# Last convolution of a four-layer network: one image loaded by nine transfers from two queues instead of three from one

## The chip, the cores and the metric

The kernel runs on one core of a Trainium2 chip. The metric is device time in microseconds (us) of one execution, as the median of several; lower is better.

## What is computed

Four layers in a row on a tensor of 8 images x 16 channels x 256 x 256 in float32; each layer adds its output to its input after a group normalisation:

```python
x = x + _L0_conv_ref(_gn(x), ...)   # 3x3 convolution, then three routing rounds
x = x + _L1_conv_ref(_gn(x), ...)   # 3x3 spline convolution
x = x + _L2_conv_ref(_gn(x), ...)   # attention over 16x16 patches
x = x + _L3_conv_ref(_gn(x), L3_conv_weight)
```

Only the last layer is touched. Its reference is written with Fourier transforms and amounts to a 3x3 convolution with circular borders, 16 channels in and 16 out, on each of the 8 images:

```python
Lw = jnp.fft.fft2(w_pad * dL)
Kx = jnp.fft.ifft2(x, norm='ortho')
z = jnp.einsum('oihw,bihw->bohw', Lw, Kx)
y = jnp.fft.fft2(z, norm='ortho')
```

## The kernel before

The layers run one after another. Layer 2 leaves each image in a DRAM scratch tensor, x3[b], with its rows padded to 258 elements (WP). Layer 3 (layer3, from L1474) loads an image into an SBUF tile of 128 partitions x 33 row groups x 258 floats, 34,056 bytes per partition, convolves it there and stores the result to the output.

Layer 3 runs over the 8 images in order, and each image in two halves, s = 0 and s = 2. A half is 384 matmuls of 32x32 weights on 512 columns (products, L1512 to L1526), each with its own weight load, all unrolled: 768 pairs of weight load and matmul per image, 6144 in the layer. The normalisation is folded into the weights ws, which weights (L1500) makes for the next image. At the end of a half ScalarE and VectorE move the sums from PSUM to a tile y (evict, L1528); y has four buffers. Then store (L1539) issues 12 or 13 transfers of a half's 2 MB, those of row blocks 0 and 1 on SyncE's queue and those of 2 and 3 on GpSimd's (L1545).

An image is loaded by fetch3 (L1466): two transfers of 16 row groups each over all 128 partitions (16,512 contiguous bytes per partition, L1471), and one small one (L1472). The first image goes into a buffer x30 during layer 2, issued by SyncE (first3, L1396, called at L1391). The other seven are issued by ScalarE (fetch, L1496). Images 1 and 2 are issued one after the other at the start of the layer (L1570, L1571). Image n + 2 takes the buffer of image n - 1, and is issued in image n between its two halves, for n = 1 to 5 (L1575, L1576). So there are three buffers: x30, named pt in the profile, and two of x3s.

The whole layer stands under manual_schedule: every engine gets its instructions in the order of the program, and an instruction that waits holds what is queued behind it on its engine. The 17 small steps of the last image's bias (todo, L1568, L1589 to L1592) are spread over the first images. Each DMA issue waits, besides for its data, for an earlier transfer that used the same one of 8 completion semaphores; SyncE and ScalarE share 8, and GpSimd has 8 of its own.

## Time and profile before

| | before |
|---|---|
| median of 3 executions | 6728.88 us (6724.0 to 6730.53) |
| the profiled execution's own time | 6725.06 us |
| its span, first to last instruction | 6723.2 us |
| granted TensorE clock, mean | 0.985 |
| TensorE matmul busy | 6116.5 us (91%), 46024 matmuls |
| VectorE, ScalarE, GpSimd busy | 5401.4, 2738.3, 3275.4 us |
| layer 3, first matmul to last weight load | 6444.6 to about 6706 us |
| moved by DMA | 800.86 MB |

Times in the profile are us from the span's start. PE is TensorE's matmul, PEld its weight load, DVE VectorE, ACT ScalarE, POOL GpSimd, SP SyncE. "issue" marks idle time in which an engine waited for nothing that the profile shows. A DMA transfer is a number of packets spread over 16 DMA engines; the queue that they came by is numbered: q1 is SyncE's, q10 ScalarE's, q0 GpSimd's (software_dynamic), and q8 carries instructions.

### The profile page before, as it was taken

Reading aid. Unit: us, or ns where it says so; the run is one execution under the profiler, and the core shown is the slowest. Engines: PE = TensorE matmul, PEld = TensorE weight load, DVE = VectorE, ACT = ScalarE, POOL = GpSimd, SP = SyncE. Lnnn points to the kernel's source line nnn. Section 1 sums busy time; section 2 is a strip of 40 time slices with the busy share of each in tenths; the row PEclk is TensorE's granted clock in tenths of the full one; section 3 lists DMA queues with packets and bytes.
Section 4 is the critical chain, followed back from the end, with each engine's and each line's share of the span. In section 5 each row is a group of like instructions: output and inputs, shape, how many; then the busy total and the mean of one; then the engine's idle time right before and its main releaser. Section 6 shows DMA issues by size and latency. Waiting matters only on the chain. (4 is left out here: it accounts for less than half of the span.)

```text
span 6723.2 us, 111466 instructions
## 1 busy us (share of the span) xinstructions
PE 6116.5 (91%) x46024; PEld 2770.6 (41%) x46024; DVE 5401.4 (80%) x6374; ACT 2738.3 (41%) x3898; POOL 3275.4 (49%) x2181
## 2 busy tenths in 40 slices
PE   3898998899899998998997799999999999999987
PEld 1333333333333333333332344444444566666654
DVE  5799999999999999999998899999999633333321
ACT  1333333333333333333332688888888421111211
POOL 0566666666666666666667333444343211111112
PEclk9999999999999999999997899999999999999999
DMA  6233333333333333333332555555556633344256
GB/s 260 61 87 91 92 91 93 88 88 94 90 90 89 88 88 88 88 88 88 88 89 60 180 176 176 175 173 178 176 175 178 174 93 80 80 102 97 81 181 213
DMA packets 372111, 800.86 MB, mean 119 GB/s; under 512 B 56210, under 2 KB 189842, under 8 KB 334354
## 3 DMA queue, kind: packets, MB, share of 16 engines
q1 hardware_dynamic: 329058, 713.30, 36.9%
q10 hardware_dynamic: 36144, 63.64, 2.6%
q0 software_dynamic: 6400, 16.78, 0.9%
q8 instruction: 361, 5.91, 0.4%
q14 instruction: 148, 1.21, 0.1%
HBM read 582.87 MB, written 210.77 MB: 118 GB/s over the span
## 5 line engine op out<-in xcount | busy, mean ns | idle before, releaser
L750 POOL TENSOR_TENSOR dd<-dd 128x1024 f32<-128x1024 f32 x512 | 1214.2, 2372 | 614.8 <-DVE dd L741 594.7
L1006 PE MATMUL ps<-bases,tw 128*32 128x512 f32 (+1 forms) x13824 | 1361.5, 545 | 16.9 <-POOL bases L975 6.5
L741 DVE SCALAR_TENSOR_TENSOR dd<-rb,v 128x1024 f32<-128x1024 f32 (+1 forms) x1024 | 1066.7, 1083 | 97.9 <-PE rb L730 90.2
L975 POOL TENSOR_TENSOR bases<-e,a 128x1024 f32<-128x1024 f32 (+1 forms) x264 | 621.8, 2379 | 928.3 <-DVE e L973 928.0
L629 DVE TENSOR_TENSOR pr<-v,fb 128x2048 f32<-128x2048 f32 (+1 forms) x512 | 1011.5, 2017 | 24.0 <-PE pl L639 12.8
L523 PE MATMUL cv<-kt,w 128*128 128x512 f32 x2048 | 1003.4, 612 | 27.4 <-DVE dd L741 21.4
L532 ACT COPY v<-cv 128x1024 f32<-128x1024 f32 x512 | 517.3, 1010 | 1154.2 <-PE cv L527 1154.2
L1006 PEld LDWEIGHTS ps<-bases,tw 128*32 128x32 f32 x13824 | 599.0, 109 | 800.8 <-issue 483.2
L750 POOL TENSOR_TENSOR s<-s,dd 128x512 f32<-128x512 f32 x512 | 671.3, 1311 | 35.1
L730 PE MATMUL rb<-rs,ct_fold 32*128 32x512 f32 x3584 | 608.7, 649 | 72.1 <-ACT rs L712 68.0
L750 POOL TENSOR_TENSOR s<-v,dd 128x512 f32<-128x512 f32 x256 | 330.7, 1292 | 660.0 <-DVE dd L741 660.0
L639 PE MATMUL pl<-pr,ct_fold 128*32 128x512 f32 x3584 | 532.5, 607 | 117.4 <-DVE pr L629 117.4
L527 PE MATMUL cv<-kt,w 64*128 64x512 f32 x2048 | 578.8, 641 | 0.0
L523 PEld LDWEIGHTS cv<-kt,w 128*128 128x128 f32 x2048 | 354.9, 191 | 524.7 <-issue 299.8
L1430 ACT ACTIVATE vt<-pv,w_b2v 128x128 f32<-128x128 f32 x512 | 146.5, 368 | 842.3 <-PE pv L1426 842.3
L1419 PE MATMUL pqk<-w_qk,t 128*128 128x512 f32 x1024 | 482.7, 594 | 4.6 <-POOL t L1413 4.6
L1451 DVE TENSOR_TENSOR y<-po,res 128x512 f32<-128x512 f32 x128 | 88.5, 692 | 490.9 <-PE po L1446 471.9
L983 DVE SCALAR_TENSOR_TENSOR bases<-xr,xm,bases 128x1024 f32<-128x1024 f32 (+1 forms) x264 | 447.8, 1734 | 0.3 <-POOL bases L975 0.3
L1413 POOL TENSOR_TENSOR t<-t,emb 128x512 f32<-128x512 f32 x128 | 162.3, 1268 | 507.1 <-DVE t L1409 496.4
L960 ACT ACTIVATE sq<-a 128x1024 f32<-128x1024 f32 (+1 forms) x264 | 263.8, 999 | 230.1 <-DVE a L952 229.3
L730 PEld LDWEIGHTS rb<-rs,ct_fold 32*128 32x128 f32 x3584 | 172.8, 185 | 416.3 <-issue 217.7
L942 ACT ACTIVATE d<-xr,bd,sd 128x1024 f32<-128x1024 f32 (+1 forms) x264 | 319.1, 1209 | 14.4 <-DMA xr<-x1p 14.4
(258 smaller groups left out, 8419.4 us busy)
## 6 DMA issues: line engine op xcount, KB each, us to landing
kt<-d SPq DMA_DIRECT2D x256, 516.0 KB
xr<-x1p SPq DMA_DIRECT2D x120, 1024.0 KB
d<-dn ACTq DMA_DIRECT2D x64, 516.0 KB
x<-y SPq DMA_DIRECT2D x128, 258.0 KB
xs<-in_x_dram SPq DMA_DIRECT2D x16, 2048.0 KB
xs<-in_x_dram SPq DMA_DIRECT2D x64, 512.0 KB
res<-in_x_dram SPq DMA_DIRECT2D x64, 512.0 KB
x<-s SPq DMA_DIRECT2D x128, 256.0 KB
```

What stands on the lines that cost most here:

```text
L523: nc.tensor.matmul(ps()[:, n], w[:, 0, j, :], t[:, a : a + 2, 0:W], start=True, stop=False)
L527: nc.tensor.matmul(ps()[:, n], w[at, 1, j, :], t[at, a : a + 2, 2 - n : 2 - n + W], start=False, stop=True)
L532: nc.scalar.copy(v[h]()[:, 4 * g : 4 * g + 4, j * W : j * W + W], ps().rearrange("p n (a w) -> p (n a) w", w=W),)
L629: nc.vector.tensor_tensor(pr()[:, :n].rearrange("p n (r w) -> p n r w", w=W), v[h]()[:, 4 * g : 4 * g + n].rearrange("p n (r w) -> p n r w ...
L639: nc.tensor.matmul(pl()[at : at + 32], sel[:, g, h, :], pr()[:, t, :], start=h == 0 and g == 0, stop=h == 1 and (g == 1 or t == 3),)
L730: nc.tensor.matmul(r()[:, n], spread[at, g, h, :], rs()[at], start=True, stop=True)
L741: nc.vector.scalar_tensor_tensor(dd()[:, :n], r()[:, :n], 1.0 / B, v[h]()[:, a : a + n], ALU.subtract, ALU.mult)
L750: op("POOL", us, lambda: nc.gpsimd.tensor_tensor(out[0](), a[0](), b[0](), ALU.add), a[1] + b[1], out[1])
L975: nc.gpsimd.tensor_tensor(ring[n % 3][:, 0, p : p + m, 1 : 1 + W], rows(e), rows(a), ALU.subtract)
L983: nc.vector.scalar_tensor_tensor(r, rows(part[1]), xm[:, b : b + 1], v, ALU.is_gt, ALU.mult)
L1006: nc.tensor.matmul(out if k is None else out[:, k], lhs, rhs, start=start, stop=stop, skip_group_check=True)
L1419: nc.tensor.matmul(ps, t[:, n, k * P : (k + 1) * P], wqk[:, n, :], start=n == 0, stop=n == 1)
```

## The change

fetch3 takes a list of engines and a range of pieces. An image is now eight transfers of 4 row groups each (4,128 contiguous bytes per partition) and the small one, piece i issued by engine i mod 2 of SyncE and GpSimd, so SyncE issues four and the small one and GpSimd four. first3 uses SyncE alone, for all nine. At the start of layer 3 only image 1 is issued. Image n + 2 is issued inside image n, for n = 0 to 5: pieces 0 to 3 behind the stores of half s = 0, pieces 4 to 8 behind the stores of half s = 2. Image 2 is among these. ScalarE issues no transfer any more in layer 3. The matmuls, the evictions, the stores, the buffers and the bytes are the same.

```diff
-    def fetch3(self, engine, b, xs):
+    def fetch3(self, engines, b, xs, part=range(9)):
         rows = self.x3[b].rearrange("r c h k w -> (r c) (h k w)")
         at = xs.rearrange("p g w -> p (g w)")
-        for k in range(0, 32 * WP, 16 * WP):
-            engine.dma_start(out=at[:, k : k + 16 * WP], in_=rows[:, k : k + 16 * WP])
-        engine.dma_start(out=at[:32, 32 * WP :], in_=rows[:32, :WP])
+        n = 4 * WP
+        for i in part:
+            engine = engines[i % len(engines)]
+            if i < 8:
+                engine.dma_start(out=at[:, i * n : (i + 1) * n], in_=rows[:, i * n : (i + 1) * n])
+            else:
+                engine.dma_start(out=at[:32, 32 * WP :], in_=rows[:32, :WP])
...
-            def fetch(b, xs):
-                self.fetch3(nc.scalar, b, xs)
-                return xs
+            loads = [nc.sync, nc.gpsimd]
...
-                for b in images[1:3]:
-                    xs.append(fetch(b, io.tile([P, 33, WP], F32, name="x3s")))
+                for b in images[1:2]:
+                    xs.append(io.tile([P, 33, WP], F32, name="x3s"))
+                    self.fetch3(loads, b, xs[1])
                 for n, b in enumerate(images):
                     for s in (0, 2):
                         y = io.tile([P, 2, 2, 4, W], F32, name="y3", bufs=4)
-                        if s and n and n + 2 < len(images):
-                            xs.append(fetch(images[n + 2], xs[n - 1]))
+                        if n + 2 < len(images) and not s:
+                            xs.append(xs[n - 1] if n else io.tile([P, 33, WP], F32, name="x3s"))
...
                         store(b, s, y)
+                        if n + 2 < len(images):
+                            self.fetch3(loads, images[n + 2], xs[n + 2], range(4, 9) if s else range(4))
```

More of the change, by code (lines that the diff above doesn't have):

```diff
@@ L1396, in first3 @@
     def first3(self, b):
-        self.fetch3(self.nc.sync, b, self.x30.rearrange("p (g w) -> p g w", w=WP))
+        self.fetch3([self.nc.sync], b, self.x30.rearrange("p (g w) -> p g w", w=WP))
     def stats3(self, bank, name):
```

## The prediction

> **What bounds the kernel now.** The change touches only the last 280 us, so I read the waits of the window 6440 to 6724 us first. TensorE lost 6.1 us to the first weights (L1502), which the change leaves alone, and 30.7 us in 21 gaps that nothing in the profile explains:

> ```profile
> PE p L1519 <- issue: 30.7, 21, 2.8
> PE p L1519 <- DVE ws L1502: 6.1, 1, 6.1
> ```

> No wait for a load of an image, a store or a PSUM buffer is among them: loads are in time already, and bandwidth as such bounds nothing. The timeline of TensorE in image 5 (6620 to 6652 us) shows the form of the gaps:

> ```profile
> 6619.50 9.93 PE L1519 MATMUL p<-x3s,ws 32*32 32x512 f32 x287
> 6630.42 4.47 PE L1519 MATMUL p<-x3s,ws 32*32 32x512 f32 x128 [0.99 <-issue]
> 6636.64 4.47 PE L1519 MATMUL p<-x3s,ws 32*32 32x512 f32 x128 [1.74 <-issue]
> 6643.40 4.67 PE L1519 MATMUL p<-x3s,ws 32*32 32x512 f32 x128 [2.29 <-issue]
> 6648.79 2.35 PE L1519 MATMUL p<-x3s,ws 32*32 32x512 f32 x65 [0.72 <-issue]
> ```

> TensorE stops after exactly 128 matmuls. With its weight loads that is 256 instructions, and the page says what comes in such lots:

> ```profile
> PE 6116.5 (91%) x46024; PEld 2770.6 (41%) x46024; DVE 5401.4 (80%) x6374; ACT 2738.3 (41%) x3898; POOL 3275.4 (49%) x2181
> ...
> q8 instruction: 361, 5.91, 0.4%
> ```

> 2 x 46024 instructions over 361 packets are 255 each, and 5.91 MB over 361 are 16 KB: every q8 packet is one block of TensorE's program. A stop is a block that came late. The windows of an image with a load (image 5) and one without (image 6) give the price:

> ```profile
> 6616.50:6649.30 32.80, 27.06 (x804) 15.87 (x794) 6.11 (x9) 6.06 (x10) 6.94 (x13) 1.00 0.76 261
> 6649.30:6676.30 27.00, 26.23 (x800) 15.78 (x770) 6.11 (x9) 4.88 (x8) 6.94 (x13) 1.00 0.58 158
> ```

> The same matmuls take 32.8 us beside a load (first column, length; the last two, DMA share and GB/s) and 27.0 us without. So the layer is bound by instruction fetch behind data packets, and at most about 6 us per loaded image can be won.

> Lining up the DMA records of q8 with the starts of the blocks gives a law. The fetch of a block begins L us after TensorE started the block before it; its packet takes 0.95 us, and TensorE resumes 1.2 to 1.5 us later. So a block takes the larger of L + 2.3 us and TensorE's own 3.6 to 4.3 us, and a stop begins at L = 2. Measured L in layer 3: 0.9 to 1.2 us with nothing in flight; 3.6 to 4.1 us behind 16.5 KB packets of q10 alone; 4.1 to 5.5 us behind these and stores; 3.4 to 4.3 us when a half's stores have just begun on q0 and q1; 1.2 to 2.0 us in their tail. Elsewhere, q1 loads alone: 8 KB packets of layer 1 median 2.05 us (16 blocks), 4 KB packets 1.3 us (2 blocks only).

> [...] So small pieces should let the fetch in sooner; the L of 1.3, 2.05 and 3.9 us for 4, 8 and 16 KB agree, growing by 0.6 to 0.75 us per 4 KB over a base near 0.7. [...]

> **The change part by part.**
> *Issues.* ScalarE loses 21 issues (L1471, L1472, 0.33 to 1.29 us each); it idles 105.9 us ahead of L1537, so 0. SyncE gets 35 in layer 3 and nine instead of three in first3; GpSimd gets 28, at the 0.54 us mean of L1545 15 us, against 217.8 us idle. Behind them in both queues stand the next half's stores, some 14 us later: 0; without that cover each would push the stores by about 1 us per half. In layer 2 SyncE's nine issues stand ahead of the stores L1462, one per 8.8 us with three buffers, and the ninth waits for the first to land: 0. TensorE's waits for pieces cost semaphore instructions: 51 ns each (L1519, 12 now); 3 to 6 more per image, 1 to 2 us in all. I take 1.
> *Waits.* A load of image n + 2 waits for image n - 1's matmuls, over half an image before. Image 2, moved behind the stores of image 0, has a whole image's time (about 30 us) for 14.9 us of transfer (q10, 6495.8 to 6510.7 beside stores). Image 1 is issued at the same 6444 as now. Cost 0.
> *Start of the layer.* Image 0's six blocks take 7.5, 5.9, 6.5, 7.9, 7.1 and 3.8 us, sum 38.7, with two images (8.5 MB) in one burst of 22 us. After: the first 6.9 (a cold TensorE at granted clock 0.74 needs nearly that by itself), the second 4.4 and third 4.3 beside one image in 4 KB packets (L 1.3 to 2), then a half like those below (15.6): 31.2, a gain of 7.5.
> *Images 1 to 5.* Now 33.3, 32.8, 32.9, 34.2 and 33.1 us, mean 33.3. A half is exactly three blocks, and its first starts with the stores. After, the first meets stores and is as now with L 3.8: 6.1. The second starts 6 us into the burst, when the stores' tail and the pieces on q1 and q0 are in flight. The trace has no load on q0. From below, L is 1.8 (the sum of 0.6 for 4 KB and a base of 1.1), so the block is 4.3. From above, q0's pieces behave like the stores there (4 KB packets of about 270 ns in the first 3 us of a burst): L 3.8, 6.1. I take L 2.8, block 5.1, [...]. The third meets the end of the load (3.1 us of stores and loads at 370 GB/s left after 8 us of the 4.1 MB): 4.2 to 4.8, I take 4.4. A half 15.6, an image 31.2: 2.05 less, times five is 10.
> *Images 6 and 7*: no loads, unchanged; nor is the tail after the last matmul.
> Sum: -7.5 - 10 + 1 = -16.5, say 17 us. The profiled execution would go from 6725.06 to 6708; the median shown stands 3.8 us above it, so 6728.88 - 17 = 6712.

> **The rivals.**
> *A. The fetch slips through everywhere.* Second and third blocks fall to TensorE's own 4.1: a half 14.3, an image 28.6; -4.7 x 5 - 9 = -33: 6696. For it: the 1.3 us of 4 KB packets. Against: only two such blocks, with one queue.
> *B. q0's pieces act like q0's stores.* Second block 6.1, third 4.8: a half 17, an image 34; +0.7 x 5, image 0 -3: 0 to +1 us: 6729. The long stops are cut up, and there are more of them. For it: L is 3.4 to 4.3 us behind stores of 2 and 4 KB packets, so packet size is not all. [...]
> *C. Slower: the spread leaves no clear block.* Now a load is one burst of 10 to 15 us and two or three blocks per image meet an idle DMA (L 0.9 to 1.2). If 4.1 MB per half keeps all 16 DMA engines busy through the half, and L stays at 4 with both queues deep, six blocks take 6.3: 37.8, +4.5 x 5 = +22, image 0 as now: 6751. It decides from a mean L of 3.2 us, where six blocks make 33.3.
> *D. The change does nothing it says* can't be for the queues: the instruction order shows the pieces behind the stores.

> **How the numbers follow.** Forecast (-8 to -26 us) 0.50, A 0.20, B 0.22, C 0.08. A measurement of this kernel can tell about 0.2%, 13.5 us, from no change. Of the forecast's half, 0.35 lies beyond that and 0.15 within; with A, faster 0.55; with B, same 0.37; C, slower 0.08. The range goes from A's lower side, 6692, to 6736, B with its spread; C and the far end of A (all images at 27 us, -40) are left out.

> **What would show it.** In the profile after: q10 gone from layer 3; the 30.7 us of "issue" gaps ahead of L1519 down to some 18 to 22, none over 2 us in images 1 to 5 but at the start of a half; the windows of such images at 31 us, image 0 near 31. I am wrong if L behind q0's loads is above 3.2 us, if stops come at every 128 matmuls, or if TensorE waits for a piece of an image.

## The result and the profile after

The changed kernel takes 6742.59 us (median of 13 runs, 6733.72 to 6747.25) against 6728.88 us for the kernel before on the same chip (13 runs, 6719.78 to 6737.82): a ratio of 1.0019, 95% interval [1.0011, 1.0028]. It is 13.7 us slower, where 17 us less had been forecast, and lies 6.6 us above the range.

The profiled execution of the changed kernel happens to be the fastest of its 13 (6733.72 us, span 6731.9), so it understates the loss. The waits of TensorE from 6440 us on (us in total, times, longest), first the kernel after, with the gaps and the first weights (6.1 us as before):

```profile
PE p L1521 <- issue: 31.6, 21, 3.1
PE p L1521 <- DVE ws L1504: 6.1, 1, 6.1
```

Then the same view of a second profile of the same code (the run e6 below, 6741.49 us), which is typical of the median:

```profile
PE p L1521 <- issue: 39.7, 28, 4.1
```

The unexplained gaps have not gone down from 30.7 us to 18 to 22; there are as many or more. No wait for a piece of an image has appeared. The DMA queues of the page after (packets, MB, share of 16 engines) show that the loads moved as meant: the 33.82 MB left on q10 all flow before layer 3.

```profile
q1 hardware_dynamic: 334290, 728.33, 37.5%
q0 software_dynamic: 10432, 31.58, 1.7%
q10 hardware_dynamic: 33792, 33.82, 1.5%
q8 instruction: 361, 5.91, 0.4%
```

TensorE's timeline of the kernel after, in images 4 and 5, still has stops ahead of lots of 128 matmuls:

```profile
6606.24 15.73 PE L1521 MATMUL p<-x3s,ws 32*32 32x512 f32 x384 [3.10 <-issue]
6623.70 4.50 PE L1521 MATMUL p<-x3s,ws 32*32 32x512 f32 x127 [1.73 <-issue]
6630.03 4.47 PE L1521 MATMUL p<-x3s,ws 32*32 32x512 f32 x128 [1.83 <-issue]
6634.87 4.67 PE L1521 MATMUL p<-x3s,ws 32*32 32x512 f32 x128 [0.37 <-issue]
```

SyncE's and GpSimd's timelines say what lies beside them. First SyncE: six stores, and the pieces behind them:

```profile
6612.83 8.44 SPq L1547 DMA_DIRECT2D out_dram<-y  x6
6621.37 1.88 SPq L1474 DMA_DIRECT2D pt<-x  x2
6628.55 6.37 SPq L1547 DMA_DIRECT2D out_dram<-y  x6
6635.02 3.08 SPq L1474 DMA_DIRECT2D pt<-x  x2
```

GpSimd does the same at the same time:

```profile
6613.39 3.24 POOL L1547 DMA_DIRECT2D out_dram<-y  x6 [13.32 <-DVE ws L1504]
6616.62 1.13 POOL L1474 DMA_DIRECT2D pt<-x  x2
6629.10 3.73 POOL L1547 DMA_DIRECT2D out_dram<-y  x7 [11.36 <-DVE y L1537]
6632.82 0.57 POOL L1474 DMA_DIRECT2D pt<-x  x1
```

So from image 0 to image 5 every half is followed by stores on both queues and then by half a load on both. The last pieces, those of image 7, go out behind the second half of image 5 and flow while image 6 is computed. Images 5 and 6 of the kernel after as windows (length, busy time of PE, PEld, DVE, ACT, POOL, then PEclk, DMA share, GB/s):

```profile
6624.90:6658.20 33.30, 28.19 (x779) 16.50 (x784) 6.11 (x9) 4.88 (x8) 9.18 (x17) 0.95 0.76 229
6658.20:6689.30 31.10, 26.72 (x781) 14.42 (x782) 6.11 (x9) 4.88 (x8) 8.05 (x15) 1.00 0.87 273
```

The prediction shows a window of image 6 before, with 27.00 us at 158 GB/s; here the image takes 31.10 us at 273 GB/s.

Cut into eight equal lots of matmuls, images 1 to 5 take 174.4 us in this profile and 174.6 in the second, against 165.9 and 165.3 in two profiles of the kernel before: about 9 us more, where 10 less had been forecast.

What was in flight while each block of images 1 to 5 waited for the fetch of the next one, counted in two profiles of the kernel before (first and e12) and two after (first and e6), 60 blocks each. L is the prediction's: from the start of a block to the fetch of the next. A kind of transfer counts if more than 40 KB of it were in flight between 0.3 us after the block's start and the fetch:

| in flight | before: blocks | with a stop after | mean L, us | gaps, us | after: blocks | with a stop after | mean L, us | gaps, us |
|---|---|---|---|---|---|---|---|---|
| nothing | 15 | 0 | 0.8 | 0 | 9 | 0 | 0.8 | 0 |
| a load alone | 10 | 10 | 4.2 | 15.5 | 13 | 2 | 1.7 | 1.5 |
| stores alone | 24 | 8 | 2.5 | 8.5 | 16 | 13 | 3.1 | 10.6 |
| a load and stores | 11 | 9 | 4.6 | 20.9 | 22 | 21 | 4.1 | 39.5 |

The change did remove the stops beside a load alone. It paid for them with twice as many blocks that meet a load and stores together.

The gaps alone do not make up the layer's loss. The whole layer as one window, before:

```profile
6444.70:6705.80 261.10, 230.24 (x6198) 132.29 (x6203) 48.99 (x88) 42.12 (x68) 51.96 (x97) 0.95 0.70 238
```

And after:

```profile
6449.40:6716.70 267.30, 235.46 (x6197) 134.61 (x6203) 49.32 (x88) 41.91 (x68) 67.31 (x125) 0.92 0.75 232
```

The layer is 6.2 us longer. Only 0.9 us of it are gaps (30.7 to 31.6); 5.2 us are busy time of the same matmuls, and the granted clock fell from 0.95 to 0.92. Windows of 4 us around one stop of the kernel after (6602 to 6606 holds the stop) show why:

```profile
6602.00:6606.00 4.00, 1.15 (x35) 0.24 (x24) 0.00 (x0) 2.09 (x2) 0.00 (x0) 0.95 0.97 319
6606.00:6610.00 4.00, 3.76 (x64) 1.32 (x66) 0.00 (x0) 0.00 (x0) 0.00 (x0) 0.50 0.74 295
6610.00:6614.00 4.00, 4.00 (x112) 2.11 (x97) 3.00 (x3) 0.00 (x0) 0.61 (x2) 0.69 0.02 6
6614.00:6618.00 4.00, 4.00 (x142) 3.14 (x127) 0.32 (x2) 0.32 (x2) 3.75 (x7) 1.00 0.92 245
```

After the stop the clock is 0.50 and 64 matmuls pass in 4 us where 142 pass later. In the clock records of layer 3 such stretches last 3.4 or 6.8 us in these two profiles (up to 10.2 us in e6) and sum to 26.6 us before and 40.2 us after. In each profile all stretches of layer 3 begin on one grid of 3.41 us, and whether one begins goes with how busy TensorE was in the window of that grid just before. In the 19 profiles other than e14's, all 60 windows at full clock in which TensorE was busy for less than 47% were followed by half clock, and none of the 1087 in which it was busy for 68% or more; of the 125 between, 29 were. So where a stop falls in the grid counts as well as its length: after the change, stops of 1.2, 1.5 and 1.8 us were followed by half clock, and one of 2.6 us was not. Over the same 19 profiles TensorE's busy time in the layer rises by 0.52 us for each us at half clock (correlation 0.93). A stop thus costs more than its gap, and this was in no step of the prediction.

### The profile page after: what moved, and what is told of

Read it like the earlier page. It is cut to its first block, busy times and chain, and to the rows that moved or that the text cites. A ratio compares the mean times of both kernels' runs of the same rounds, so it can differ in the third digit from the quotient of the medians.

```text
span 6731.9 us, 111575 instructions
## 1 busy us (share of the span) xinstructions
PE 6124.9 (91%) x46024; PEld 2774.4 (41%) x46024; DVE 5402.3 (80%) x6374; ACT 2738.1 (41%) x3898; POOL 3292.1 (49%) x2209
## 3 DMA queue, kind: packets, MB, share of 16 engines
q10 hardware_dynamic: 33792, 33.82, 1.5%
q8 instruction: 361, 5.91, 0.4%
```

## The experiments

The layer's length is from its first to its last weight load, "issue" is the idle time of TensorE ahead of its weight loads and the number of gaps, PE is TensorE's busy time in the layer, all from one profile each. The ratio is to the kernel before on the same chip.

| run | loads: queue, piece | stores: queue | median us (less before) | ratio [95%] | layer us | issue us / gaps | PE us |
|---|---|---|---|---|---|---|---|
| before | ScalarE, 16.5 KB bursts | SyncE + GpSimd | 6728.88 | | 261.2 | 30.7 / 21 | 230.2 |
| after | SyncE + GpSimd, 4 KB | SyncE + GpSimd | 6742.59 (+13.7) | 1.0019 [1.0011, 1.0028] | 267.4 | 31.6 / 21 | 235.5 |
| e6 (after again) | the same | the same | 6741.49 (+12.0) | 1.0017 [1.0009, 1.0024] | 274.7 | 39.7 / 28 | 234.9 |
| e1 | SyncE, 4 KB | SyncE + GpSimd | 6725.87 (-5.6) | 0.9992 [0.9986, 0.9999] | 259.8 | 29.6 / 26 | 229.9 |
| e2 | ScalarE, 4 KB | SyncE + GpSimd | 6732.96 (+1.5) | 1.0002 [0.9994, 1.0011] | 263.4 | 32.6 / 28 | 230.5 |
| e5 | GpSimd, 4 KB | SyncE + GpSimd | 6741.46 (+12.0) | 1.0019 [1.0011, 1.0026] | 270.4 | 38.0 / 21 | 232.4 |
| e8 | ScalarE, 4 KB, paced | SyncE + GpSimd | 6739.67 (+10.2) | 1.0014 [1.0007, 1.0020] | 268.1 | 32.3 / 23 | 235.6 |
| e3 | ScalarE, 4 KB bursts | SyncE + GpSimd | 6732.09 (+0.6) | 1.0000 [0.9992, 1.0008] | 262.4 | 23.8 / 19 | 230.6 |
| e4 | none | SyncE + GpSimd | 6694.31 (-37.2) | 0.9942 [0.9928, 0.9955] | 229.2 | 13.0 / 11 | 216.3 |
| e7 | SyncE, 4 KB | SyncE | 6714.71 (-14.8) | 0.9974 [0.9965, 0.9984] | 244.8 | 21.3 / 15 | 223.4 |
| e11 | SyncE, 16.5 KB | SyncE | 6716.08 (-11.6) | 0.9982 [0.9975, 0.9988] | 250.6 | 23.4 / 18 | 226.4 |
| e9 | ScalarE, 16.5 KB bursts | SyncE | 6715.68 (-12.0) | 0.9983 [0.9974, 0.9991] | 243.1 | 17.7 / 17 | 225.1 |
| e10 | SyncE + GpSimd, 4 KB | SyncE | 6708.84 (-18.9) | 0.9972 [0.9960, 0.9983] | 244.8 | 19.4 / 15 | 225.2 |
| e15 | GpSimd, 4 KB | SyncE | 6708.91 (-20.2) | 0.9974 [0.9962, 0.9985] | 238.4 | 18.5 / 16 | 219.9 |
| e18 | GpSimd, 16.5 KB bursts | SyncE | 6717.19 (-14.4) | 0.9979 [0.9970, 0.9987] | 246.8 | 18.1 / 13 | 228.6 |
| e13 | ScalarE, 16.5 KB bursts | GpSimd | 6720.23 (-8.9) | 0.9988 [0.9980, 0.9996] | 249.6 | 22.7 / 18 | 226.8 |
| e16 | SyncE, 4 KB | GpSimd | 6715.58 (-13.6) | 0.9980 [0.9971, 0.9988] | 243.5 | 20.7 / 17 | 222.7 |
| e17 | ScalarE, 16.5 KB bursts | SyncE, then GpSimd | 6723.13 (-8.5) | 0.9987 [0.9980, 0.9993] | 247.6 | 21.1 / 17 | 226.2 |
| e14 | ScalarE, 16.5 KB bursts | SyncE + ScalarE | 6782.41 (+53.3) | 1.0079 [1.0066, 1.0093] | 317.4 | 9.5 / 7 | 248.4 |

**The scatter: e6 and e12.** The changed kernel (e6) and the kernel before (e12) once more, with no edit.

> The changed kernel once more, unaltered, on the chip of these runs, since its one profile was the fastest of its 13 runs. Both theories: 1.001 to 1.003 of the time before; if the profile taken so far understates its layer 3, it takes 268 to 275 us here, and layers 0 to 2 start layer 3 at 6444 to 6455 us as in all other runs.

> The kernel before once more, for the scatter of its profile: every theory expects the layer at 258 to 268 us (261.2 in the first profile), its start at 6444 to 6457 us, and the idle time of TensorE ahead of its weight loads at 28 to 36 us.

e12 gave a layer of 260.6 us (261.2 in the first profile), issue 30.9 us in 19 gaps, and one time of 6737.89 us. Its layer starts at 6458.3 us, that of the first profile at 6444.7, though nothing before it differs: this start scatters by 14 us, so a profile's span is a worse witness than its layer. In e6 the layer is 7 us longer than in the first profile of the change. The sign of the loss is sure; its size in one profile is good to some 7 us.

**Which queue carries the loads: e1, e2, e5.** The changed kernel with one line edited: `[nc.sync]` in e1, `[nc.scalar]` in e2, `[nc.gpsimd]` in e5.

```diff
-            loads = [nc.sync, nc.gpsimd]
+            loads = [nc.sync]
```

> The changed kernel with all nine pieces of an image on SyncE's queue q1, at the same places; nothing of a load on GpSimd's queue q0. Layer 3 from its first to its last weight load took 261.2 us before and 267.4 us after the change. Queue theory (TensorE's instruction fetch is held by packets of q0, and the change put half of each load there): the fetch delays fall to those of stores and 4 KB pieces on q1, layer 3 takes 245 to 256 us, 10 us or more less than after, and the run is 5 to 15 us faster than before. Spread theory (any load spread behind the stores makes nearly every block of instructions meet traffic, whatever the queue): 264 to 270 us, as after, and about 10 us slower than before.

> The changed kernel with the nine pieces issued by ScalarE, on q10, at the same places. Queue theory: as with SyncE alone, 245 to 256 us for layer 3 and 5 to 15 us faster than before; a little better or worse than SyncE alone, since q10's pieces do not stand behind the stores of q1. Spread theory: 264 to 270 us, as after.

> The changed kernel with all nine pieces of an image on GpSimd's queue q0 and none on SyncE's: twice the change's dose of q0. Layer 3 takes 261.2 us before, 267.4 us with the change, 259.8 us with SyncE alone. Queue theory (pieces on q0 hold TensorE's instruction fetch longer than the same pieces on q1): slower than the change, layer 3 at 272 to 285 us, 20 us or more slower than before in time. Spread theory (a fetch waits about 3.5 us behind any saturated traffic, and the queue is a side matter): 258 to 268 us, no slower than the change.

e2 keeps the queue of before and takes only the pieces and their spread from the change: +1.5 us, within the uncertainty. So spreading small pieces brings nothing by itself. e1 leaves GpSimd's queue out and is 17 us or more faster than the change; e5 puts all there and is as slow as the change with half of them. What the change lost, compared with e1, it lost by loads on GpSimd's queue, behind the stores there. No layer came out in the range of either theory, though: 259.8, 263.4 and 270.4 us lie between the two each time.

**Pacing the pieces: e8.** One piece behind each quarter of a half's matmuls, from ScalarE, held back by a copy there; image 1 from SyncE alone. ScalarE takes over copies of VectorE.

```diff
+                                i = 2 * s + 2 * q + k
+                                if n + 2 < len(images):
+                                    self.fetch3(loads, images[n + 2], xs[n + 2], range(i, i + 1 + (i == 7)))
...
-                        if n + 2 < len(images):
-                            self.fetch3(loads, images[n + 2], xs[n + 2], range(4, 9) if s else range(4))
```

> One piece of an image at a time: ScalarE issues piece after piece, each behind a quarter of a half's matmuls (its copies or evictions of that quarter pace it), so the pieces do not stand in one burst behind the stores; image 1 is issued by SyncE. If a fetch waits for the bytes queued ahead of it, one piece of 33 KB per DMA engine (1.2 us) is below the 2 us that are hidden: stops only behind stores, layer 3 takes 238 to 248 us, 10 to 20 us faster than before. If any transfer in flight costs a fetch 3.5 us, 258 to 266 us.

It is 10.2 us slower than before, and its layer is longer than either theory had it. In images 1 to 5, 17 of 30 blocks meet a load and the stores of both queues (4 and 6 in the two profiles before), with a mean L of 4.0. Its gaps are those of e2 (32.3 us against 32.6), its busy time is 5.1 us longer, with 32.6 us at half clock against 21.1. So thinning the loads out makes more blocks meet a load with stores and does not shorten the gaps.

**The size of a piece: e3 and e11.** e3 is the kernel before with bursts of eight transfers of 4 KB per partition in place of two of 16.5 KB; e11 is e7 (below) with 16.5 KB in place of 4 KB.

```diff
-        for k in range(0, 32 * WP, 16 * WP):
+        for k in range(0, 32 * WP, 4 * WP):
```

> The kernel before with its loads cut into eight pieces of 4 KB per partition, still on ScalarE's queue and at the old places and times: the size of the pieces alone. If the delay of a fetch grows with the size of the packets before it, as I forecast (3.9 us at 16 KB, 1.3 us at 4 KB), the stops beside a load go and layer 3 takes 240 to 250 us, 10 to 20 us faster than before. If size does not matter beside the number of packets queued, 259 to 263 us, as before.

> All loads and stores on SyncE as in the run before of that kind, but each image in three transfers of up to 16 KB per partition in place of eight of 4 KB. If the size of a piece doesn't matter for the fetches, the layer takes 242 to 250 us and the run is 12 to 16 us faster than before, as with pieces of 4 KB. If small pieces let fetches through, the layer takes over 252 us and the run gains less than 8 us.

e3's gaps fell from 30.7 to 23.8 us, but its 18 issues at the start of the layer kept ScalarE from a copy, and TensorE waited for it:

```profile
PE p L1519 <- issue: 23.8, 19, 2.3
PE p L1519 <- ACT seen L1585: 7.7, 1, 7.7
```

A fetch may have arrived during that wait of 7.7 us too, so the fall in e3's gaps can't be put down to the size alone. e11 has gaps of 23.4 us against 21.3 in e7, and its gain is 11.6 us against 14.8, with intervals that overlap; its layer of 250.6 us is just over the range for a size that doesn't matter. So the size counts for a few us. Over all profiles, beside a load alone that flows on after the fetch, L is 3.2 us behind 4 KB pieces (72 blocks, 47 of them with a stop) and 4.0 us behind 16.5 KB (41 blocks, 37 stops). Where the load is ending, L is 1.6 us behind 4 KB (42 blocks, 3 stops) and 3.2 us behind 16.5 KB (16 blocks, 8 stops). A fourth of the size thus goes with a fifth less L while a load flows, and with half of it where the load is ending.

**What loads cost at all: e4.** The kernel before without the loads of images 1 to 7: the first image's tile stands in for them.

```diff
-                            xs.append(fetch(images[n + 2], xs[n - 1]))
+                            xs.append(xs[0])
```

> The kernel before with the loads of images 1 to 7 left out: every image is convolved from the buffer of image 0. All theories: no stop but behind stores, images of 27 us, the first some 30: layer 3 takes 215 to 225 us, about 40 us faster than before. This is the floor that any way of loading has. If it is above 240, the stops are not made by loads and both theories fall.

It is 37.2 us faster. The layer is 32.0 us shorter (229.2 us, a little over the 215 to 225 expected), and some 5 us more come from ahead of it: the first weights no longer wait for the last transfer of layer 2, and TensorE waits 0.8 us for them in place of 6.1. In the layer 13.0 us of gaps in 11 stops remain, each with stores of both queues in flight (L 2.8 to 5.1). So the loads are most of what can be won, but the stores alone stop TensorE too, which the prediction had priced and then left as it was.

In e4's waits this stands in place of the 6.1 us for the weights:

```profile
PE p L1519 <- DVE y L1451: 0.8, 1, 0.8
```

**One queue for the stores: e7, e9, e10.** In all three the stores go to SyncE; the loads are those of e1 (e7), of before (e9), and of the change (e10).

```diff
-                    (nc.sync if c < 2 else nc.gpsimd).dma_start(
+                    nc.sync.dma_start(
```

> The changed kernel with every piece and every store of layer 3 on SyncE's queue, nothing on GpSimd's: q0 is empty. Queue theory in its strong form (packets of q0 are what holds a fetch, the stores' own too): delays behind stores drop from 3 to 5 us to below 2, layer 3 takes 235 to 250 us, 10 us or more faster than before. Spread theory: delays stay at 3.5 us behind stores and pieces, 255 to 265 us. SyncE issues 16 or 17 transfers per half, at 0.5 to 1 us each.

> The kernel before with one edit: all stores of the last convolution are issued by SyncE, none by GpSimd; the loads stay two transfers of 16.5 KB per partition from ScalarE. If what GpSimd's queue carries is the cost, and neither the spread nor the size of the loads matters, the layer takes 240 to 250 us (before 261.2, all on SyncE with small pieces 244.8), the idle time of TensorE ahead of its weight loads 18 to 24 us, and the run is 10 to 15 us faster than before. If the spread or the small pieces help once that queue is empty, the layer takes 252 to 260 us and the run gains at most 8 us.

> The changed kernel with one edit: all stores on SyncE, the pieces still on SyncE and GpSimd in turn, so that GpSimd's queue carries half of the pieces alone. If every transfer on GpSimd's queue holds the fetches back, the layer takes 255 to 265 us, some 10 to 20 us more than with everything on SyncE (244.8), and the run is within 5 us of before. If only stores on that queue do it, the layer takes about 245 us and the run is 14 us faster than before.

That edit makes the kernel before 12 us faster and the changed kernel about 31 us faster (e10 stands 18.9 us below before, the change 12.0 to 13.7 above it). e10 also refutes the theory that I held until then, that GpSimd's queue is bad for whatever it carries: half of the pieces still go there, and with no stores beside them on that queue they cost nothing (the layer takes 244.8 us, as in e7 with every piece on SyncE). SyncE's timeline in e9 shows what became of the stores:

```profile
6639.54 50.49 SPq L1545 DMA_DIRECT2D out_dram<-y  x56
```

That is 50.49/56 = 0.9 us per issue, short waits included (the issues by themselves take 0.82 us in the mean), so a half's 12 or 13 stores (2.1 MB) are stretched over 10 to 12 us, and over up to 24 us with longer waits between them. Windows of 2 us, before, at the stores of a half in image 6 with no load about (the last column is GB/s):

```profile
6656.00:6658.00 2.00, 2.00 (x80) 1.39 (x59) 0.32 (x2) 0.00 (x0) 1.86 (x4) 1.00 0.91 246
6658.00:6660.00 2.00, 2.00 (x84) 1.56 (x68) 0.00 (x0) 0.00 (x0) 0.00 (x0) 1.00 1.04 299
6660.00:6662.00 2.00, 1.93 (x69) 0.86 (x59) 0.00 (x0) 1.58 (x2) 0.00 (x0) 1.00 0.94 244
```

And in e9:

```profile
6656.00:6658.00 2.00, 2.00 (x81) 1.32 (x59) 0.16 (x1) 0.00 (x0) 0.00 (x0) 1.00 0.93 206
6658.00:6660.00 2.00, 2.00 (x82) 1.56 (x68) 0.00 (x0) 1.27 (x2) 0.00 (x0) 1.00 0.67 156
6660.00:6662.00 2.00, 2.00 (x77) 1.38 (x63) 0.04 (x1) 0.85 (x1) 0.00 (x0) 1.00 0.92 199
```

**GpSimd's queue, or two queues at once: e13, e14, e15, e16, e17, e18.** e13 puts all stores of the kernel before on GpSimd, e14 half on SyncE and half on ScalarE. e15 and e16 are the change with each queue carrying one kind: stores on SyncE and pieces on GpSimd (e15), and the reverse (e16). e18 is e9 with the loads of before issued by GpSimd. All are edits of the store line above and of the loads' list. e17 keeps both store queues of before, and only holds GpSimd's part back until ScalarE's eviction in the next half:

```diff
+                                    if k == 0 and late:
+                                        nc.gpsimd.tensor_copy(mark, y[:, 0, 0, 3, W - 2 : W])
+                                        store(*late.pop(), cs=(2, 3))
...
-                        store(b, s, y)
+                        store(b, s, y, cs=(0, 1))
+                        late.append((b, s, y))
```

> The kernel before with all stores of the last convolution on GpSimd's queue, the loads as before on ScalarE's. If GpSimd's queue as such holds the fetches back, the layer takes 261 to 272 us and the run is no faster than before. If what counts is that one queue carries the stores at a lower rate than two (150 to 200 GB/s in place of 380), the layer takes 240 to 250 us, as with all stores on SyncE (243.1), and the run is 10 to 15 us faster than before.

> The kernel before with the stores on SyncE and ScalarE in place of SyncE and GpSimd: two queues at once, but none of them GpSimd's. If GpSimd's queue as such is the cost, the layer takes 240 to 250 us. If two queues that fill the DMA engines at once are the cost, the layer takes 258 to 268 us and the time is within 5 us of before, beside any wait of TensorE for ScalarE's copies (seen), whose instructions now stand behind ScalarE's issues and which is to be counted apart.

> The changed kernel with all stores on SyncE and all pieces on GpSimd: each queue carries one kind. If loads on GpSimd's queue cost fetches, the layer takes 252 us or more, over the 244.8 of the run with pieces on both queues. If only the stores' two queues do it, the layer takes 240 to 248 us and the run is 15 to 20 us faster than before.

> The mirror of it: the changed kernel with all stores on GpSimd and all pieces on SyncE. If GpSimd's queue as such holds the fetches back, the layer takes 261 us or more. If what counts is that one queue alone carries the stores, at a lower rate, the layer takes 240 to 250 us and the run is 12 to 20 us faster than before.

> The kernel before, with each half's stores still on two queues, but those on GpSimd's queue set some 8 to 10 us later by a copy of two values that waits for ScalarE's eviction in the next half; loads as before. If the cost is that the stores of two queues run at the same time, the layer takes 243 to 252 us and the run is 8 to 15 us faster than before. If two queues as such, or GpSimd's, are the cost, the layer takes 258 to 268 us and the time is within 4 us of before.

> The kernel before with all stores on SyncE and its loads, two transfers of 16.5 KB per partition in one burst at the places of before, issued by GpSimd in place of ScalarE. If spreading the loads in pieces is what brought the run with pieces on GpSimd from 6715.7 (bursts on ScalarE) to 6708.9 us, the layer takes 242 to 248 us and this run is at about 6715 us. If the loads' queue did it, the layer takes 236 to 241 us and the run is at about 6709 us.

e13 and e16 are faster than before by 8.9 and 13.6 us with *all* stores on GpSimd (e13's gain is a little under the 10 us expected), so that queue as such isn't the cost. e17 has both queues and GpSimd's stores, only for the most part at different times. GpSimd's timeline in e17:

```profile
6617.52 0.18 POOL L1586 COPY mark<-y 128x2 f32<-128x2 f32 x1 [13.00 <-ACT y L1537]
6618.10 3.24 POOL L1545 DMA_DIRECT2D out_dram<-y  x6 [0.40 <-issue]
6632.97 0.19 POOL L1586 COPY mark<-y 128x2 f32<-128x2 f32 x1 [11.64 <-ACT y L1537]
6633.52 3.81 POOL L1545 DMA_DIRECT2D out_dram<-y  x7 [0.36 <-issue]
```

The stores of the two queues are in flight together for 37 us of the layer, against 91 us before. Its layer takes 247.6 us, as expected of the theory that the time counts (243 to 252), and not the 258 to 268 of the other:

```profile
PE p L1519 <- issue: 21.1, 17, 2.6
```

The mean rate at which stores flow falls with it, from 218 to 185 GB/s in images 6 and 7, so e17 alone doesn't tell the two apart. e13 does in part: it gains with one queue at 207 GB/s. So what holds the fetches back is, for the most part, stores of two queues at the same time. e14 settles nothing: TensorE waited 59.3 us for ScalarE's copies, which stood behind stores in ScalarE's queue, as its waits show; in the slack of those waits few fetches were late (9.5 us of gaps):

```profile
PE p L1519 <- ACT seen L1585: 59.3, 15, 6.1
```

e15 and e10 are the fastest of the versions that load, some 31 to 34 us below the change. In e15 the pieces are hardly spread any more: GpSimd has nothing else to wait for, so it issues one piece and then, when TensorE's matmuls release the rest, seven at once (3.64 us, here for an image loaded into pt):

```profile
6565.61 0.55 POOL L1474 DMA_DIRECT2D pt<-x  x1 [13.22 <-PE p L1521]
6579.87 3.64 POOL L1474 DMA_DIRECT2D pt<-x  x7 [13.70 <-PE p L1521]
```

Its images 6 and 7, with stores on SyncE alone, no longer lose anything: TensorE is busy throughout (window, length, PE busy).

```profile
6638.80:6664.30 25.50, 25.50 (x788) 18.26 (x776) 6.11 (x9) 4.93 (x9) 0.00 (x0) 1.00 0.75 168
6664.30:6690.00 25.70, 25.70 (x795) 19.21 (x779) 5.58 (x8) 4.88 (x8) 0.00 (x0) 1.00 0.76 173
```

e18, the same queues with bursts of 16.5 KB, expected at 6715 us if the spread or the pieces brought the last 7 us and at 6709 if the queue did, came to 6717, 14.4 us under the kernel before on its chip, where e9 is 12.0 and e15 20.2 under it: the queue did not. The queues being equal, it is the size of the pieces or the moment of the burst; these were not taken apart.

All blocks of layer 3 in the 20 profiles, by what was in flight up to the fetch (counted as above; a load flows on if more than 100 KB of it start in the us after the fetch; other mixtures are left out):

| in flight | blocks | of these with a stop after | mean L, us |
|---|---|---|---|
| nothing | 195 | 1 | 0.9 |
| stores of SyncE alone | 197 | 21 | 1.8 |
| stores of GpSimd alone | 48 | 10 | 2.0 |
| stores of both | 147 | 98 | 3.0 |
| 4 KB pieces alone, ending | 42 | 3 | 1.6 |
| 4 KB pieces alone, flowing on | 72 | 47 | 3.2 |
| 16.5 KB pieces alone, ending | 16 | 8 | 3.2 |
| 16.5 KB pieces alone, flowing on | 41 | 37 | 4.0 |
| stores of both, 4 KB pieces on ScalarE's queue | 27 | 22 | 4.0 |
| stores of both, 4 KB pieces on GpSimd's queue | 22 | 20 | 4.5 |

## Why the prediction was wrong

*What bounds the layer* was right: instruction fetch behind data. Taking the loads away shortened the layer by 32 us, gaps never came from a wait for a piece, and stops still come at blocks of 128 matmuls.

*The step that failed* is the second block of a half, where GpSimd's pieces meet the stores. The prediction took L 2.8 there, an estimate between bounds of 1.8 and 3.8. Measured in images 1 to 5, the blocks that meet pieces and stores together have L 4.1, and 21 of 22 stop; over all profiles, stores of both queues with pieces on GpSimd's have L 4.5, above both ends. Stores of both queues alone have 3.0 and 4 KB pieces alone 1.6 to 3.2: the two add up, they don't replace each other. An L above 3.2 us behind GpSimd's loads was also the prediction's own first sign of being wrong. This term has the wrong sign: images 1 to 5 went up by about 9 us instead of down by 10.

*The law's entry for small pieces*, "L 1.3 to 2", came from two blocks of 4 KB and 16 of 8 KB in layer 1; that small pieces let the fetch in sooner was an estimate from these few blocks and the 3.9 us behind 16 KB. (Its lower bound of 1.8 for the second block adds 0.6 to a base of 1.1, where the law itself has a base near 0.7; the difference decides nothing.) As a law it failed: with pieces that flow on, L is 3.2 us, and 2.5 to 3.0 in the first two blocks of image 0 after the change. In images 1 to 5 it came true all the same, since the blocks that meet pieces alone meet mostly the end of a load: L is 1.7 there, and 2 of 13 blocks stop. They still took 6.2 us in the mean and not the 4.4 forecast for the third block of a half, with TensorE at half clock in 10 of the 13, after the stop before them.

*A missing term* is TensorE's clock after a stop. Busy time rose by 5.2 us in the first profile at nearly equal gaps (0.9 us more); in the second by 4.6 us, with 9 us more of gaps. It fits the 13.6 us more at half clock in the first, which at a granted clock of 0.50 can cost at most half of that, 6.8 us, and the 9.4 us in the second. In images 1 to 5 alone, busy time is 7.3 us of the rise in the first profile and gaps are 1.2; in the second, against e12, they are 4.3 and 5.5.

*Image 0*, forecast at -7.5: 39.4 and 36.0 us in two profiles before, 34.4 and 36.8 after. The gain, if any, is within that scatter. *Issues and waits* at no cost held: GpSimd's and SyncE's pieces wait at times, TensorE for none. The microsecond for its semaphores can't be told from the rest.

*Images 6 and 7*, forecast unchanged because they have no load: 55.8 and 59.3 us before, 58.6 and 63.3 after. The prediction overlooked that the change moves the last pieces of image 7 behind the second half of image 5, and so into image 6. That image took 26.7 and 28.3 us before, 31.1 and 31.4 after, and the window above shows the traffic. The other runs agree as far as their scatter allows: with this spread (e1, e2, e5) the two images take 61 to 64 us, with loads that end in image 5 (e3, e8) or none (e4) 55 to 58. *The tail* after the last weight load fell from 17.3 to 15.1 us, which no step had.

*The sum*: over two profiles each the layer went from 260.9 to 271.1 us and the tail from 17.3 to 15.1, +8.0 us; the medians say +12.0 to +13.7. The 4 to 6 us between are within the scatter of one profile's layer and of its start, and are not assigned.

*The rivals*: A (all fetches slip through) is refuted by the 34.9 us of an image. B is nearest in mechanism: GpSimd's pieces act like its stores, and its image of 34 us is close to the 34.9. It priced the whole at 6729, without the clock, image 6 and the scatter of image 0. C, given 0.08, is nearest in time (6751) but not in mechanism, so that is luck: 17 and 21 of 30 blocks in images 1 to 5 stop, not all, and the mean L there is 2.7 and 2.9 us, under the 3.2 from which C decides (before: 2.7 and 2.8). D is refuted by the queues. All rivals changed the loads; none asked what the stores beside them cost as they were, which is where 12 to 20 us lay.

*Settled*: with stores on two queues the size of the pieces and their spread bring nothing that the medians show (e2, e3); with stores on one queue they may bring 3 to 6 us, with overlapping intervals (e7 against e11, e15 against e18). The loss comes with loads on GpSimd's queue beside stores on both (e1, e5 against e6); it goes, with 12 to 20 us more, when stores no longer run on two queues at once (e9, e10, e15, e17). *Open*: why pieces behind GpSimd's stores are worse than on ScalarE's queue (L 4.5 against 4.0, in few blocks); why two queues delay a fetch more than one; and whether in the stores the rate or the number of queues counts more. GpSimd alone moves them at up to about 280 to 300 GB/s, as both do, and has L 2.0 against 3.0, so the number counts; SyncE alone at some 200 GB/s has 1.8, so the rate adds little. The two queues also differ in the size of their packets (2 KB on SyncE's, 4 KB on GpSimd's), and no run varied that.

## What to carry to other kernels

Where an unrolled stretch uses up a block of instructions in about 4 us, look at which blocks meet which transfers: here it counted more how many blocks met loads and stores of several queues at once than how large a piece was, and spreading a load over time only made more blocks meet both (22 of 60 in images 1 to 5 after the change, 11 of 60 before). Give each kind of transfer one queue (8.9 to 20.2 us faster than before in e9, e13, e15, e16 and e18), and let the issuing engine's own pace thin out the stores (0.82 us per issue on SyncE in e9); here one line was worth 12 us on the kernel before and about 31 on the changed one. A delay law measured beside light traffic didn't hold here beside bursts (L 1.3 to 2 us expected behind small pieces, 3.2 measured where they flow on), and a stop is to be priced with the slow clock after it (here 0.52 us of busy time for each us at half clock).
